# A graph layer's gather: one tile of rows in 104 fetched by SyncE row by row, the others by GpSimd

## The chip, the cores and the metric

The kernel runs on one core of a Trainium2 chip. The metric is the device time of one execution in microseconds (us); lower is better. Of a core's engines the profile names PE (TensorE, with PEld for its weight loads), DVE (VectorE), ACT (ScalarE), POOL (GpSimd) and SP (SyncE). SP computes nothing here: its queue (SPq in the profile) issues transfers.

## The reference

One layer of a graph network over 12500 nodes with 96 features and 412500 edges that are sorted by their destination node. For each edge a message is formed from the source node's features, the destination node's features and the edge's own four attributes; the messages are normalized over all edges and summed by destination node.

```python
def _mlp(h, W, b, gamma, beta):
    h = relu(h @ W + b)
    mu, var = mean(h, axis=0), mean(square(h - mean(h, axis=0)), axis=0)
    return gamma * (h - mu) * rsqrt(var + 1e-5) + beta

node_feat = _mlp(x, W_node, b_node, g_node, beta_node)
edge_feat = _mlp(edge_attr, W_edge, b_edge, g_edge, beta_edge)
message = _mlp(concat([x[src], x[dst], edge_feat], axis=1), W_msg, b_msg, g_msg, beta_msg)
agg = segment_sum(message, dst, num_segments=12500)
x = layernorm(x + agg + node_feat)
```

## The kernel before

**Tables.** The product with `W_msg` splits into three parts. `table` (L144) computes the source part for every node once into a table `p_tab` in HBM, one row of 96 floats (384 bytes) per node, and the destination part into `q_tab`. So an edge needs only its row of `p_tab`, a row of `q_tab` and its edge part.

**Tiles, groups and blocks.** 128 edges are a tile (one partition per edge), four tiles a group (`GT = 4`), four groups a block (`BG = 4`): 3223 tiles, 806 groups, 202 blocks.

**Gathers.** `gather` (L162) fetches the `p_tab` rows of a group: one indirect DMA of GpSimd for each tile, whose 128 row numbers lie in the column `src[:, k]`, one per partition (L166). The groups of the first 26 blocks (`SPILL = 104` groups, called early) are gathered while the tables and the edge statistics are worked out, and are spilled to HBM. The other 702 groups (late) are gathered into a ring of `RING = 28` tiles named `pg`; the first 28 before the main loop, every further one 28 late groups ahead of its use, at the end of the loop's step (`ahead_of`, L332 and L526).

**The main loop** (from L503) has a step for each group, in an order that puts one early block between every few late ones. The order of the instructions on SP, POOL, PE, DVE and ACT is the program's (L496). In each step `linear` (L447) multiplies the edge and destination part on PE, `message` (L455) adds the gathered rows to it on DVE (L465: `hs<-z,pg`), which is also the last use of a ring tile, and ACT applies the relu; `sums` and `add` collect the messages by node.

**What SP does in the loop.** At the first step of each block SP runs `load(s + 2)` (L387), two blocks ahead: every second block five transfers of edge attributes (L396, L397), and for each block one number read from the tile `base` into a register (L400) and two transfers of rows of `q_tab` at the address that this register gives, into one of three buffers `rhs` (L405). These two wait until PE has read that buffer for the last time. For an early block `fetch` (L408) brings its spilled rows back (L412).

Of the kernel before, what the change touches and what calls it, by code (L numbers as in the profile page):

```python
# [11 lines left out]
F32 = mybir.dt.float32  # L12
I32 = mybir.dt.int32
# [3 lines left out]
ET = mybir.EngineType  # L17
# [3 lines left out]
N, C, E, ED = 12500, 96, 412500, 4  # L21
EPS = 1e-5
P = 128
# [3 lines left out]
GT, GE, BG = 4, 512, 4  # L27
NT = -(-E // P)
NG = -(-NT // GT)
NBL = -(-NG // BG)  # L30
NTP, NGP = NBL * BG * GT, NBL * BG
EP = NGP * GE
# [23 lines left out]
SPILL = 26 * BG  # L56
RING = 28
RAW = 3
SKEW = 6
HB, RB = 3, 3  # L60
CL, CE = 2, 2
J = 8


# [12 lines left out]
def gnn(ctx, tc, t):  # L77
    nc = tc.nc
    const = ctx.enter_context(tc.tile_pool(name="const", bufs=1))
    dram = ctx.enter_context(tc.tile_pool(name="dram", bufs=1, space=DRAM))  # L80
    p_tab = dram.tile([NN, C], F32, name="p_tab")
# [11 lines left out]
    ring = rpool.enter_context(tc.tile_pool(name="ring", bufs=RING))  # L93
# [65 lines left out]
            queues[c // CH % len(queues)].dma_start(rows[:, c:c + CH, :], r)  # L159
            yield  # L160

    def gather(g, pg):  # L162
        tab, idx = (t["x"], src_raw) if g < RAW * BG else (p_tab, src)
        for i in range(min(GT, NT - g * GT)):
            k = g * GT + i
            nc.gpsimd.indirect_dma_start(  # L166
                out=pg[:, i, :], out_offset=None, in_=tab[:, :],
                in_offset=bass.IndirectOffsetOnAxis(ap=idx[:, k:k + 1], axis=0))
        return pg
# [107 lines left out]
    def edge_norm():  # L277

        with tc.tile_pool(name="es", bufs=2) as work, tc.tile_pool(name="es1", bufs=1) as one, \
                tc.tile_pool(name="es_ps", bufs=4, space=PSUM) as ps:  # L280
            stats = one.tile([P, NS, NBL, 6], F32, name="estats")
            for b in range(NBL):
                if b % J == 0:
                    yield
                    ea = work.tile([P, J, GE], F32, name="ea")
                    n = min(J, NBL - b)
                    for i in range(NS):
                        nc.sync.dma_start(ea[Q * i:Q * i + 2 * EK, :n, :],
                                          t["ea"][EK * i:EK * (i + 2), b:b + n, :])
                for i in range(NS):  # L290
                    k = NS * b + i
                    if k % 2 == 0:
                        pr = ps.tile([P, 2, GE], F32, name="pr")
                    nc.tensor.matmul(pr[:, k % 2, :], wide[Q * i:Q * i + 2 * EK, :],  # L294
                                     ea[Q * i:Q * i + 2 * EK, b % J, :], start=True, stop=True)
                    if k % 2:
# [32 lines left out]
            nc.vector.tensor_scalar(w_e, w_msg[:, 2, :], a_e, None, op0=OP.mult)  # L329

    def fast(ring):
        def ahead_of(g):  # L332
            return gather(g, ring.tile([P, GT, C], F32, name="pg"))

        with tc.manual_schedule(engines={ET.SP, ET.Pool}):
            with tc.tile_pool(name="tab_w", bufs=1) as work, tc.tile_pool(name="tab_ps", bufs=2, space=PSUM) as ps:
# [20 lines left out]
            got = {g: ahead_of(g) for g in range(SPILL, SPILL + RING)}  # L357
# [11 lines left out]
        with tc.tile_pool(name="fix", bufs=1) as fix, tc.tile_pool(name="msg", bufs=2) as work, \  # L369
# [17 lines left out]
            def load(s):  # L387

                b = order[s]
                first = SPILL // BG  # L390
                c, o = ((b - first) // CL * CL + first, CL) if b >= first else (b // CE * CE, CE)
                if c not in eas:
                    o = min(o, NBL - c)
                    eas[c] = work.tile([P, o, GE], F32, name="ea" if b >= first else "eae")
                    for i in range(BG):
                        nc.sync.dma_start(eas[c][Q * i:Q * i + EK, :, :], t["ea"][EK * i:EK * (i + 1), c:c + o, :])  # L396
                    nc.sync.dma_start(eas[c][EK:P:Q, :, :], rel_d[:, c * BG * GE:(c + o) * BG * GE]  # L397
                                      .rearrange("o (b g e) -> (o g) b e", g=BG, e=GE))
                ea = eas[c][:, b - c, :]
                _, val = nc.values_load_multi_w_load_instructions(  # L400
                    base[:, b:b + 1], engines=[ET.SP], min_val=0, max_val=N - 1,
                    skip_runtime_bounds_check_because="they are nodes' numbers")
                for i in range(2):
                    rows = q_tab[WS * i:, :][bass.ds(val[0], 4 * WS), :].rearrange("(k w) f -> w k f", k=2)
                    nc.sync.dma_start(rhs[C:C + WN, s % RB, i::2, :], rows[:WN])  # L405
                block[s] = ea

            def fetch(s):  # L408
                b = order[s]
                if b * BG < SPILL:  # L410
                    back = work.tile([P, BG, GT, C], F32, name="pb")
                    nc.sync.dma_start(back, spill[b].rearrange("p g (a c) -> p g a c", a=GT))  # L412
                    for i in range(BG):
                        got[b * BG + i] = back[:, i, :, :]
# [18 lines left out]
            def edges(s):  # L433

                prs[s] = ps.tile([P, BG, GE], F32, name="pr", bufs=1)
                for i in range(min(BG, NG - order[s] * BG)):
                    nc.tensor.matmul(prs[s][:C + WN, i, :], we[Q * i:Q * i + EK + 1, :],  # L437
                                     block[s][Q * i:Q * i + EK + 1, :], start=True, stop=True)

            def prepare(s):  # L440

                n = min(BG, NG - order[s] * BG)
                pr, x = prs[s], left[s % 2]
                nc.scalar.activation(x[:C, :n, :], pr[:C, :n, :], AF.Relu)  # L444
                nc.vector.tensor_scalar(x[C:C + WN, :n, :], pr[C:C + WN, :n, :], 0.0, None, op0=OP.is_equal)  # L445

            def linear(k):  # L447
                s, g = steps[k]
                n = min(GT, NT - g * GT)
                zs[k] = ps.tile([P, GT, C], F32, name="z")  # L450
                for i in range(n):
                    nc.tensor.matmul(zs[k][:, i, :], left[s % 2][:KR, g % BG, i * P:(i + 1) * P],  # L452
                                     rhs[:KR, s % RB, g % BG, :], start=True, stop=True)

            def message(k):  # L455
                g = steps[k][1]
                n = min(GT, NT - g * GT)
                i = g % BG
                h, z, pg = hb[k // 2 % HB], zs.pop(k), got.pop(g)
                if i % 2 == 0:  # L460
                    nc.vector.tensor_tensor(  # L461
                        h[:, :, :, C + 1:C + 1 + WN], rel[:, g:g + 2, :].unsqueeze(3).to_broadcast([P, 2, GT, WN]),
                        iota[:, i:i + 2, :].unsqueeze(2).to_broadcast([P, 2, GT, WN]), op=OP.is_equal)
                hs = work.tile([P, GT, C], F32, name="hs", bufs=3)
                nc.vector.tensor_add(hs[:, :n, :], z[:, :n, :], pg[:, :n, :])  # L465
                nc.scalar.activation(h[:, i % 2, :n, :C], hs[:, :n, :], AF.Relu)  # L466

            def sums(k):

                s, g = steps[k]  # L470
                n = min(GT, NT - g * GT)
                h = hb[k // 2 % HB][:, g % 2, :, :]
                if g % BG == 0:
                    pas[s] = ps.tile([C + 1, BG, P], F32, name="pa")
                for i in range(n):
                    r = min(P, E - (g * GT + i) * P)
                    nc.tensor.matmul(pas[s][:, g % BG, :C + 1 + WN], h[:r, i, :C + 1], h[:r, i, :C + 1 + WN],  # L477
                                     start=i == 0, stop=i == n - 1)

            def add(s):  # L480
# [9 lines left out]
                    nc.vector.tensor_tensor(to, pa[:, i:n:2, C + 1:C + 1 + WN], to, op=OP.add)  # L490
                nc.vector.tensor_add(gram[:, :n, :], pa[:, :n, :C + 1], gram[:, :n, :])  # L491

            n, ahead = len(steps), SPILL + RING
            with tc.manual_schedule(engines={ET.SP, ET.Pool, ET.PE, ET.DVE, ET.Activation}):  # L496
                load(0)
                fetch(0)
                load(1)
                edges(0)  # L500
                prepare(0)
                linear(0)
                for k in range(n + SKEW):  # L503
                    s, g = steps[min(k, n - 1)]
                    if k < n and g % BG == 0:
                        if s + 2 < len(order):
                            load(s + 2)
                        if s + 1 < len(order):
                            fetch(s + 1)
                    if k + 1 < n:  # L510
                        linear(k + 1)
                    if k < n:
                        message(k)
                    if 0 <= k - 1 < n:
                        sums(k - 1)
                    if k < n and s + 1 < len(order):
                        if g % BG == 0:
                            edges(s + 1)
                        if g % BG == 2:
                            prepare(s + 1)  # L520
                        if g % BG == 3 and order[s + 1] < RAW:
                            convert(s + 1)
                    if k >= SKEW and (k - SKEW) % BG == 0:
                        add((k - SKEW) // BG)
                    if k < n and g >= SPILL and ahead < NG:
                        got[ahead] = ahead_of(ahead)  # L526
                        ahead += 1

            d = fix.tile([C, BG, C], F32, name="d")
            s = fix.tile([C, 3], F32, name="s")  # L530
# [237 lines left out]
```

## Time and profile before

| | us |
|---|---|
| median of 3 runs | 5475.15 |
| lowest and highest of them | 5470.85 to 5479.21 |
| the profiled execution, its own time | 4143.65 |
| its span in the profile | 4141.9 |
| mean granted TensorE clock in it | 0.764 |

All durations below are of the one profiled execution, whose own time is 1331.5 us below the median. A row of the table of groups names a line, an engine, an operation and `out<-in`, then how often it ran, its busy time, the mean of one in ns, the idle time of its engine ahead of it and what ended most of that. "issue" there is time in which the engine waited for nothing that the profile shows. In a list of waits, "A <- B: t, n, m" says that A waited for B t us in total, n times, at most m us. An answer about one line gives count and the shortest, median and longest duration in ns, then the first and last start in us.

### The profile page before, as it was taken

How to read it: one execution, taken by the hardware profiler on the slowest of the kernel's cores; microseconds unless marked ns; L12 is line 12 of the kernel's file. 1: busy time of each engine (PE TensorE's matmuls, PEld its weight loads, DVE VectorE, ACT ScalarE, POOL GpSimd, SP SyncE). 2: the span in 40 equal slices, each digit the busy share in tenths (PEclk: the TensorE clock that was granted, in tenths of full speed). 3: DMA queues.
4: the chain of work that ended last, by engine and by line, in shares of the span. 5: the costliest groups of instructions: out<-in, count | busy, mean ns of one | idle time of the engine just before them, and what ended most of it. 6: DMA issues, size and time to landing. Idle time of an engine off the chain costs nothing. (4 is left out here: it accounts for less than half of the span.)

```text
span 4141.9 us, 48307 instructions
## 1 busy us (share of the span) xinstructions
PE 2736.8 (66%) x16705; PEld 2333.7 (56%) x16705; DVE 1715.8 (41%) x2837; ACT 1144.4 (28%) x1417; POOL 3063.0 (74%) x3231
## 2 busy tenths in 40 slices
PE   6699976777566656666565656655666565665666
PEld 6466645666456545555555555555555555555556
DVE  2579993444333333333333333332333333333334
ACT  0358862223222222222122222221222122222222
POOL 7677777777777777777777777777777777777772
PEclk9755556889778878877788777877877788877785
DMA  6455542222221222122212221222212212222123
GB/s 212 140 142 113 113 81 56 54 55 55 53 53 46 53 53 54 46 53 53 52 47 53 52 54 45 53 54 52 55 45 54 52 46 55 53 52 53 46 52 108
DMA packets 154615, 270.89 MB, mean 65 GB/s; under 512 B 83665, under 2 KB 84178, under 8 KB 153356
## 3 DMA queue, kind: packets, MB, share of 16 engines
q0 software_dynamic: 103136, 158.62, 16.2%
q1 hardware_dynamic: 48138, 98.39, 8.1%
q10 hardware_dynamic: 3088, 10.71, 0.8%
q8 instruction: 134, 2.20, 0.2%
q14 instruction: 119, 0.97, 0.1%
HBM read 225.88 MB, written 41.60 MB: 65 GB/s over the span
## 5 line engine op out<-in xcount | busy, mean ns | idle before, releaser
L166 POOL DMA_INDIRECT pg<-p_tab,src x2807 | 2662.4, 948 | 856.5 <-issue 705.9
L452 PE MATMUL z<-rhs,left 128*128 128x96 f32 x6446 | 1111.9, 329 | 1246.2 <-issue 1145.0
L452 PEld LDWEIGHTS z<-rhs,left 128*128 128x128 f32 x6446 | 1016.7, 240 | 1458.0 <-issue 1325.0
L466 ACT ACTIVATE h<-hs 128x384 f32<-128x384 f32 x806 | 421.3, 523 | 2613.7 <-DVE hs L465 2613.7
L465 DVE TENSOR_TENSOR hs<-z,pg 128x384 f32<-128x384 f32 x702 | 389.2, 554 | 1558.1 <-DMA pg<-p_tab,src 1308.9
L477 PE MATMUL pa<-h 128*97 128x128 f32 x6446 | 1026.0, 312 | 4.1 <-ACT h L466 4.1
L477 PEld LDWEIGHTS pa<-h 128*97 128x97 f32 x6446 | 913.4, 198 | 4.5 <-ACT h L466 4.5
L445 DVE TENSOR_SCALAR left<-pr 31x2048 f32<-31x2048 f32 x202 | 463.0, 2292 | 487.2 <-ACT left L444 487.2
L166 POOL DMA_INDIRECT stage<-p_tab,src x368 | 350.6, 953 | 131.9 <-issue 109.7
L444 ACT ACTIVATE left<-pr 96x2048 f32<-96x2048 f32 x202 | 374.0, 1851 | 16.1 <-PE pr L437 16.1
L294 PE MATMUL pr<-ea,wide 10*128 10x512 f32 x1212 | 361.4, 1073 | 9.4 <-issue 7.8
L300 DVE BATCH_NORM_STATS2 estats<-r 128x6 f32<-128x512 f32 x606 | 360.2, 676 | 9.3 <-ACT r L298 9.3
L298 ACT ACTIVATE r<-pr 128x1024 f32<-128x1024 f32 x303 | 301.9, 1024 | 113.0 <-PE pr L294 76.8
L294 PEld LDWEIGHTS pr<-ea,wide 10*128 10x128 f32 x1212 | 223.0, 314 | 146.5 <-issue 69.4
L437 PE MATMUL pr<-ea,we 6*127 6x512 f32 x1404 | 202.5, 645 | 12.2 <-DMA ea<-rel_d 12.2
L461 DVE TENSOR_TENSOR h<-rel,iota 128x248 f32<-128x248 f32 x403 | 164.3, 408 | 0.0
L465 DVE TENSOR_TENSOR hs<-z,pb 128x384 f32<-128x384 f32 x104 | 57.7, 555 | 133.4 <-PE z L452 133.4
L491 DVE TENSOR_TENSOR gram<-pa,gram 97x388 f32<-97x388 f32 x202 | 111.4, 551 | 0.0
L490 DVE TENSOR_TENSOR agg<-pa,agg 97x62 f32 x404 | 90.1, 223 | 14.4 <-PE pa L477 0.8
L154 PE MATMUL pt<-w_msg,xp 96*128 96x96 f32 x392 | 85.2, 422 | 13.8 <-DMA xp<-in_xp 9.3
L154 PEld LDWEIGHTS pt<-w_msg,xp 96*128 96x128 f32 x392 | 84.0, 332 | 14.8 <-issue 9.3
L437 PEld LDWEIGHTS pr<-ea,we 6*127 6x127 f32 x1404 | 55.1, 183 | 38.0 <-issue 13.1
(106 smaller groups left out, 591.5 us busy)
## 6 DMA issues: line engine op xcount, KB each, us to landing
pg<-p_tab,src POOLq DMA_INDIRECT x2807
spill<-stage SPq DMA_DIRECT2D x26, 768.0 KB
pb<-spill SPq DMA_DIRECT2D x26, 768.0 KB
ea<-in_ea SPq DMA_DIRECT2D x75, 160.0 KB
rhs<-q_tab SPq DMA_DIRECT2D x404, 23.2 KB
ea<-in_ea SPq DMA_DIRECT2D x352, 20.0 KB
stage<-p_tab,src POOLq DMA_INDIRECT x368
q_tab<-trow SPq DMA_DIRECT2D x7, 672.0 KB
```

The costliest lines, as they stand in the source:

```text
L154: nc.tensor.matmul(pt[:, g, :], xp[:, k:k + P], w, start=True, stop=True)
L166: nc.gpsimd.indirect_dma_start(out=pg[:, i, :], out_offset=None, in_=tab[:, :], in_offset=bass.IndirectOffsetOnAxis(ap=idx[:, k:k + 1], ax ...
L294: nc.tensor.matmul(pr[:, k % 2, :], wide[Q * i:Q * i + 2 * EK, :], ea[Q * i:Q * i + 2 * EK, b % J, :], start=True, stop=True)
L298: nc.scalar.activation(r, pr, AF.Relu)
L300: nc.vector.bn_stats(stats[:, (k - o) % NS, (k - o) // NS, :], r[:, 1 - o, :])
L437: nc.tensor.matmul(prs[s][:C + WN, i, :], we[Q * i:Q * i + EK + 1, :], block[s][Q * i:Q * i + EK + 1, :], start=True, stop=True)
L444: nc.scalar.activation(x[:C, :n, :], pr[:C, :n, :], AF.Relu)
L445: nc.vector.tensor_scalar(x[C:C + WN, :n, :], pr[C:C + WN, :n, :], 0.0, None, op0=OP.is_equal)
L452: nc.tensor.matmul(zs[k][:, i, :], left[s % 2][:KR, g % BG, i * P:(i + 1) * P], rhs[:KR, s % RB, g % BG, :], start=True, stop=True)
L465: nc.vector.tensor_add(hs[:, :n, :], z[:, :n, :], pg[:, :n, :])
L466: nc.scalar.activation(h[:, i % 2, :n, :C], hs[:, :n, :], AF.Relu)
L477: nc.tensor.matmul(pas[s][:, g % BG, :C + 1 + WN], h[:r, i, :C + 1], h[:r, i, :C + 1 + WN], start=i == 0, stop=i == n - 1)
```

## The change

For 25 of the late groups GpSimd gathers only the first three tiles. The fourth tile's 128 rows are fetched by SP: `row_numbers` brings the tile's 128 row numbers into one partition (`lin`), and `rows_of` reads ten of them into SP registers at a time and issues one transfer for each, from that row of `p_tab` to that row's partition of the ring tile. The ten go out at the end of every second step that gathers a group, so that a tile takes 26 groups of gathers (104 tiles): with the 674 groups gathered in the loop this happens 25 times (groups 132, 158, ..., 756), in 13 batches each (12 of ten rows, one of eight). The row numbers of the next such tile are fetched at the first batch of the one before it. A further input array `rows` holds the row numbers with a tile in each row.

```diff
+SR, SS = 10, 2
+SG = SS * -(-P // SR)
...
-    def gather(g, pg):
+    def gather(g, pg, without=0):
         tab, idx = (t["x"], src_raw) if g < RAW * BG else (p_tab, src)
-        for i in range(min(GT, NT - g * GT)):
+        for i in range(min(GT, NT - g * GT) - without):
...
+            def row_numbers(g):
+
+                lin = work.tile([1, P], I32, name="lin")
+                nc.sync.dma_start(lin, t["rows"][g * GT + GT - 1:g * GT + GT, :])
+                return lin
+
+            def rows_of(pg, lin, lo, hi):
+                _, val = nc.values_load_multi_w_load_instructions(
+                    lin[:, lo:hi], engines=[ET.SP], min_val=0, max_val=N - 1,
+                    skip_runtime_bounds_check_because="they are nodes' numbers")
+                for p in range(lo, hi):
+                    nc.sync.dma_start(pg[p:p + 1, GT - 1, :], p_tab[bass.ds(val[p - lo], 1), :])
...
             n, ahead = len(steps), SPILL + RING
+            lins = {ahead: row_numbers(ahead)}
...
                     if k < n and g >= SPILL and ahead < NG:
-                        got[ahead] = ahead_of(ahead)
+                        m = (ahead - SPILL - RING) % SG
+                        if m == 0:
+                            by_row = ahead if ahead + SG <= NG else None
+                        got[ahead] = ahead_of(ahead, int(ahead == by_row))
+                        if by_row is not None and m % SS == 0:
+                            if m == 0 and ahead + 2 * SG <= NG:
+                                lins[ahead + SG] = row_numbers(ahead + SG)
+                            lo = m // SS * SR
+                            rows_of(got[by_row], lins[by_row], lo, min(lo + SR, P))
                         ahead += 1
```

More of the change, by code (lines that the diff above doesn't have):

```diff
@@ L331, in fast, with ahead_of @@
     def fast(ring):
-        def ahead_of(g):
-            return gather(g, ring.tile([P, GT, C], F32, name="pg"))
+        def ahead_of(g, without=0):
+            return gather(g, ring.tile([P, GT, C], F32, name="pg"), without)
         with tc.manual_schedule(engines={ET.SP, ET.Pool}):
@@ L742 @@
     give("src", np.pad(s, (0, EP - E)).reshape(NTP, P).T)
+    give("rows", np.pad(s, (0, EP - E)).reshape(NTP, P))
     give("dst", d.reshape(NTP, P).T)
```

## The prediction

> **What bounds the kernel now.** I read the page's busy times first, then the groups, then the stretches of the loop, the answer for the gather's line, and last the waits of the engines and of SP's queue.
>
> ```profile
> PE 2736.8 (66%) x16705; PEld 2333.7 (56%) x16705; DVE 1715.8 (41%) x2837; ACT 1144.4 (28%) x1417; POOL 3063.0 (74%) x3231
> ...
> L166 POOL DMA_INDIRECT pg<-p_tab,src x2807 | 2662.4, 948 | 856.5 <-issue 705.9
> ```
>
> No engine looks full: POOL shows 74%. But its second row says that between two gathers (948 ns each) it stood for 856.5 / 2807 = 0.305 us and that this was mostly "issue", so nothing made it wait. The gap belongs to the gather.
>
> ```profile
> 1000.00:2000.00 1000.00, 621.62 (x4186) 552.54 (x4184) 346.90 (x581) 224.85 (x291) 756.70 (x799) 0.80 0.20 51
> 2000.00:3000.00 1000.00, 612.81 (x4104) 543.77 (x4104) 339.55 (x569) 217.34 (x283) 756.98 (x798) 0.79 0.20 52
> 3000.00:4000.00 1000.00, 611.52 (x4104) 543.05 (x4104) 342.82 (x572) 221.92 (x287) 756.40 (x799) 0.79 0.20 51
> ```
>
> The columns are the stretch, its length, the busy time of PE, PEld, DVE, ACT and POOL, the clock, the DMA engines' share and GB/s. In every 1000 us POOL makes 798 or 799 gathers, one in 1.2525 us, whatever mix of blocks falls into it. From the first start to the last in the trace, 3223 gathers take 4069.5 us, 1.263 us each; in the loop's phase the mean is 1.2536 us. PE is 61% busy and the DMA engines 20%.
>
> ```profile
> DVE hs L465 <- DMA pg<-p_tab,src: 1308.9, 331, 8.3
> ...
> POOL pg L166 <- DVE hs L465: 8.8, 29, 0.3
> ...
> SPq L405 <- PE z L452: 2814.1, 398, 26.0
> ```
>
> The consumer waits for the gather (1308.9 us) and the gather almost never for a free ring tile (8.8 us): POOL's queue sets the pace from start to end. The last gather starts at 4072.6 and the span ends at 4141.9, so 69 us follow it. SP, by the third line, stands for most of the loop.
>
> **What the skill says.** "Perfetto Trace Analysis", section DMA Optimizations, item 3: where descriptor generation is the bottleneck, balancing transfers over the engines that can issue them may help. The trace shows that case at POOL. "DMA: Bandwidth & Descriptors", Issuing engines are not separate DMA queues: all issuers share 16 DMA engines, and another issuer saves only sequencer time. That agrees with a DMA share of 0.20: room below, a full issuer above. The same page, Latency and other measured facts, gives a register load a floor of about 600 ns; the trace has 431 to 815 ns on SP. "Runtime: NRT & Kernel Launch", Instruction fetch mechanics, puts a bulk load at about 200 ns for each register, from HBM; no run here shows a load of several, and this one reads SBUF.
>
> **Removed.** 25 of the 2807 ring gathers leave POOL, the only engine without slack: 25 x 1.2536 = **31.3 us**. Nothing else moves past POOL; the gathers behind each come that much earlier, and the 69 us of tail follow. The consumer keeps pace, as PE is 61% busy.
>
> **Added on SP.** 3200 row transfers, 325 register loads of ten (25 of eight), 25 transfers of row numbers. The rows for the prices, each a count and shortest/median/longest in ns:
>
> ```profile
> L192 SPq DMA_DIRECT2D b_msg<-in_L_gnn_b_msg x1: 264/264/264, 15.7 to 15.7; - x1
> ...
> L377 SPq DMA_DIRECT2D rhs<-bias x12: 578/590/608, 629.4 to 636.4; - x12
> ...
> L405 SPq FUSED_REGOPS  x404: 42/46/51, 639.7 to 4019.8; - x135
> L405 SPq MOVE rhs<-q_tab x404: 29/29/42, 639.8 to 4020.0; - x135
> L405 SPq DMA_DIRECT2D rhs<-q_tab x404: 227/262/1016, 639.9 to 4021.3; - x135
> ...
> L400 SPq TENSOR_LOAD <-base x202: 431/680/815, 638.9 to 4008.7; - x101
> ```
>
> - A row transfer. Line 405 already issues transfers from HBM at an address from a register: 46 + 29 + 262 ns, and the trace has gaps of about 50 ns after each of the three: 0.49 us. A single 384-byte row from HBM (line 192) costs 264 ns by itself, so I take 0.49. Low end: 223 ns (line 193's transfer) and the same rest, 0.45. High end: line 377's row from SBUF to SBUF costs 590 ns, which would make 0.82. I take the first because source and address kind are the same.
> - A load of ten. Low end: as a load of one, 0.68 us. By the skill's figure 0.68 + 9 x 0.2 = 2.5 us, an estimate, which I take. High end: ten loads of one, 6.8.
> - The row numbers: 25 transfers of about 0.3 us, 8 us in all.
>
> Sum: 3200 x 0.49 + 325 x 2.5 + 8 = 1568 + 813 + 8 = **2389 us** on SP.
>
> What covers it: the batches are spread over the time from the first loop gather to group 780, 2575 gathers, or 3228 us. In the trace from 1000 to 3900 us SP waits 2428.9 of 2900 us at line 405 alone, 84%; so 0.84 x 3228 = 2704 us are free there. 2389 fit into that, at 88% of it; with the 16% that SP does now it is then (0.16 x 3228 + 2389) / 3228 = **90% busy**. The limit lies at 2704 / 3200 = 0.845 us for each row with its share of the load; my price is 0.75.
>
> Order on SP: in each block the waiting `load` comes first, then the two batches, then the next block's `load`. The batches need nothing from PE or DVE, except the first of a tile, which waits for `hs` of the group that used the ring tile before (its own step). Behind SP is the next `load`, two blocks ahead of use (some 40 us at 16 x 1.25 = 20 us for a block), so being late by less than a block delays nobody. A tile's last batch goes out four groups, about 20 us, ahead of its `hs`. Even a late row would not hold POOL: the ring is 28 groups deep, and the consumer has 39% to catch up with. So I cost the new wait of `hs` on SP's rows, and the few semaphore waits it needs (17 ns each on DVE, 25 times), at nothing; the cover is DVE's 1308.9 us of waiting. On the DMA engines 3200 packets of 384 bytes are added to 154615.
>
> **Sum for the profiled execution:** 4143.65 - 31.3 = 4112.3 us, span 4110.6. The median of the runs is 1331.5 us higher, and the profile does not say where. If that time lies outside the gathers, 31 us go (5444). If each gather is that much slower, 1.656 us, 25 x 1.656 = 41.4 us go (5434). A time that scales with the length of the kernel is easier to put into 3223 equal gathers than anywhere else I see, so I lean to the second: **5437 us**. In that reading SP also has more room, unless it is slower in the same ratio.
>
> **Rivals.**
> 1. *SP becomes the bound (slower).* Place: SP's queue in the loop. From 0.845 us for a row with its share of load, SP can't finish two batches and its `load` within a late block's 20 us; the lag adds up until `rhs` comes late and PE waits. Price at the high row end: (0.82 x 3200 + 813) - 2704 = 733 us over, or with short loads 2624 + 221 - 2704 = 141 over; in the middle about 430, less the 31. That is some 5870 us on the median's scale (5585 to 6180). For it: my own 90%, and line 377's 590 ns. Against: source and address are those of line 405, at 262 ns. 0.17.
> 2. *Rows land too slowly (slower, the same place).* SP's transfers take turns on eight completion semaphores, as the trace shows at each, and one waits for the one eight before it. If a row takes over 8 x 0.59 = 4.7 us to land, the pitch passes the limit. No wait of that kind is long now (1.9 us once). It is in the 0.17.
> 3. *Contention gives the gain back (same).* If SP's transfers stretch each of the other 2782 gathers by 31.3 / 2782 = 0.011 us, 0.9%, nothing is left: 5475. For it: some gathers do take up to 1237 ns where the median is 947. Against: the pitch holds at 1.25 us through stretches with and without SP's 768 KB transfers. 0.06.
> 4. *The change doesn't do what it says:* that the three gathers of such a group take POOL as long as four. Each gather is an instruction of its own, so I see no way.
>
> **How the numbers follow.** Faster 0.77, same 0.06, slower 0.17; 0.2% is about what a measurement of this kernel can tell from no change (11 us). The range takes the likeliest case with both scales of the gain (5434 to 5444), the spread of the runs (about 4 us either way) and partial losses up to no gain: 5420 to 5476. The slower rival is left out.
>
> **What would show it.** Right: 2782 ring gathers at an unchanged 948 ns and 0.305 us of gap; the span 31 us shorter; row transfers of about 260 ns at starts some 0.49 us apart; SP's wait at line 405 down from 2814 to some 450 us; PE's and DVE's waits of the same kinds as now. Wrong: SP's wait at line 405 near zero and new waits of PE at line 452 for `rhs` (rival 1), SP waiting for its own rows (rival 2), or gaps above 0.305 us at line 166 (rival 3). A load of ten above 3.4 us, or a row above 0.59 us, would overturn the sum; so would POOL waiting for `hs`.

## The result: 1.2% slower

| | before | after |
|---|---|---|
| median, us | 5477.18 | 5544.65 |
| lowest to highest, us | 5470.85 to 5482.49 | 5534.80 to 5552.47 |
| executions | 4 | 4 |
| ratio of after to before | | 1.0123, 95% interval 1.0104 to 1.0141 |

The change costs 67 us where I forecast a gain of 38. The profiled execution of after took 5552.47 us by its own time, with a span of 5550.7 us. It is like the other executions of its kernel. The execution of before from which I made the prediction was not: its 4143.65 us were not seen again, for all 80 other executions of that kernel took between 5407 and 5498 us. So the profile after is set beside a new profile of the unchanged kernel (the first experiment, span 5455.6 us). In the changed kernel the gather is line 168, `z` line 454, `hs` line 467, the `rhs` transfers line 407, the load of ten registers line 502 and the row transfers line 506.

From the page of after, the busy times and the gathers' row of the groups:

```profile
PE 3114.1 (56%) x16705; PEld 2511.7 (45%) x16705; DVE 1723.7 (31%) x2837; ACT 1139.3 (21%) x1417; POOL 3037.3 (55%) x3206
...
L168 POOL DMA_INDIRECT pg<-p_tab,src x2782 | 2638.4, 948 | 1957.6 <-DVE hs L467 1143.5
```

The 25 gathers are gone and one still takes 948 ns. But POOL is busy for 55% of the span, and most of what it stands idle for is now `hs`: it waits for a free ring tile. In the profile that I read, that wait was 8.8 us. (133.2 us of the 1143.5 are one wait, for the loop's first `hs`.)

The stretches of the loop of after (stretch, length, busy time and instructions of PE, PEld, DVE, ACT and POOL, clock, DMA share, GB/s):

```profile
2000.00:3000.00 1000.00, 557.87 (x3288) 474.17 (x3289) 274.45 (x459) 176.24 (x229) 593.19 (x626) 0.71 0.18 40
3000.00:4000.00 1000.00, 559.07 (x3266) 474.32 (x3265) 269.91 (x451) 175.66 (x227) 594.40 (x628) 0.70 0.18 41
```

POOL gets 626 or 628 gathers into 1000 us, not 798, and no other engine is busier for it. From the waits of the engines in after (who waited for what, us in total, times, longest):

```profile
DVE hs L467 <- issue: 1760.0, 262, 14.7
...
PE z L454 <- issue: 1300.5, 349, 19.1
POOL pg L168 <- DVE hs L467: 1143.5, 288, 133.2
...
DVE hs L467 <- DMA pg<-p_tab,src: 109.6, 40, 2.8
```

The same two lines in the profile that I read were:

```profile
PE z L452 <- issue: 1145.0, 201, 11.9
...
DVE hs L465 <- issue: 96.9, 42, 2.8
```

The consumer's wait for gathers has shrunk from the 1308.9 us of that profile to 109.6. In its place DVE stands for 1760 us, not 97, for which the profile shows no releaser at all. PE's line tells little: it was 1145 us already. SP's part of the change, asked for by line in after (count and shortest/median/longest in ns, first and last start in us), and SP's own waits:

```profile
L506 SPq MOVE pg<-p_tab x3200: 1/29/1422, 1065.6 to 5242.8; - x189
L506 SPq DMA_DIRECT2D pg<-p_tab x3200: 1/225/1407, 1065.7 to 5242.9; - x189
...
L502 SPq TENSOR_LOAD <-lin x325: 3/1207/2442, 1064.1 to 5232.5; - x163
```

```profile
SPq L407 <- PE z L454: 183.9, 45, 24.7
...
SPq L506 <- DMA pg<-p_tab: 52.9, 91, 1.4
```

A row's transfer costs a median of 225 ns, the move ahead of it 29 (but up to 1422), and a load of ten 1207; these medians are under the prices that I had put on them. Yet SP's wait for `rhs` to come free has all but gone: within a batch the starts of neighbouring rows lie a mean of 0.92 us apart (median 0.56), not the 0.49 that I forecast.

### The profile page after: what moved, and what is told of

It reads as the page before. It is cut to its first block, busy times and chain, and to the rows that moved or that the text cites. A ratio compares the mean times of both kernels' runs of the same rounds, so it can differ in the third digit from the quotient of the medians.

```text
span 5550.7 us, 58501 instructions
## 1 busy us (share of the span) xinstructions
PE 3114.1 (56%) x16705; PEld 2511.7 (45%) x16705; DVE 1723.7 (31%) x2837; ACT 1139.3 (21%) x1417; POOL 3037.3 (55%) x3206
## 5 line engine op out<-in xcount | busy, mean ns | idle before, releaser
L168 POOL DMA_INDIRECT pg<-p_tab,src x2782 | 2638.4, 948 | 1957.6 <-DVE hs L467 1143.5
L454 PE MATMUL z<-rhs,left 128*128 128x96 f32 x6446 | 1201.1, 342 | 1358.4 <-issue 1300.5
L454 PEld LDWEIGHTS z<-rhs,left 128*128 128x128 f32 x6446 | 1088.2, 252 | 1606.8 <-issue 1524.1
L479 PE MATMUL pa<-h 128*97 128x128 f32 x6446 | 1234.0, 335 | 553.8 <-issue 550.6
L479 PEld LDWEIGHTS pa<-h 128*97 128x97 f32 x6446 | 1031.3, 214 | 640.5 <-issue 639.9
L296 PE MATMUL pr<-ea,wide 10*128 10x512 f32 x1212 | 403.8, 1074 | 314.8 <-issue 220.3
L296 PEld LDWEIGHTS pr<-ea,wide 10*128 10x128 f32 x1212 | 204.8, 321 | 512.4 <-issue 340.6
L439 PE MATMUL pr<-ea,we 6*127 6x512 f32 x1404 | 229.2, 724 | 15.5 <-DMA ea<-rel_d 12.6
```

The lines of the kernel that those rows point to most:

```text
L168: nc.gpsimd.indirect_dma_start(out=pg[:, i, :], out_offset=None, in_=tab[:, :], in_offset=bass.IndirectOffsetOnAxis(ap=idx[:, k:k + 1], ax ...
```

## Experiments

Ratios are to the kernel before on the same chip, with 95% intervals. Where two experiments are compared, their ratios are, since the kernel before takes 5441 to 5487 us on different chips. What is read from a trace is one execution.

**1. The kernel before again.** No edit.

> The kernel before, unchanged, for a trace of it at the time of the median (5477 us) and not of the one execution of 4144 us that the prediction read. Theory A (in the timed executions the consumer of the gathers, not POOL, sets the pace): about 5477 us, POOL waits for DVE hs (ring tiles in use) for over 800 us in sum, and the mean distance of two gathers in the loop is near 1.6 us while single gathers still take 948 ns. Theory B (POOL sets the pace there too, each gather being slower): about 5477 us, POOL's wait for DVE hs stays under 50 us and the gather's own 948 ns or its 0.305 us gap has grown by 0.4 us.

Measured: 0.9994 (0.9972 to 1.0016), 5445 us. From the waits of its engines:

```profile
DVE hs L465 <- remote: 1447.4, 168, 15.5
...
POOL pg L166 <- DVE hs L465: 1024.2, 194, 131.7
...
PE z L452 <- issue: 856.4, 561, 9.3
```

So the unchanged kernel, too, has POOL waiting for `hs` for 1024 us (131.7 of them in one wait, for the loop's first `hs`), and DVE standing for 1447 us at a wait whose releaser the profile can't name ("remote"). What happens there is seen in its timeline (start, duration, engine, line, operation, count, and the idle time ahead with its releaser):

```profile
3030.77 1.92 PE L477 MATMUL pa<-h 128*97 128x128 f32 x8
...
3033.98 0.45 PEld L477 LDWEIGHTS pa<-h 128*97 128x97 f32 x2
3034.04 0.95 POOL L166 DMA_INDIRECT pg<-p_tab,src  x1 [0.31 <-issue]
...
3034.95 0.37 PE L477 MATMUL pa<-h 128*97 128x128 f32 x1 [0.40 <-issue]
...
3035.66 0.37 PE L477 MATMUL pa<-h 128*97 128x128 f32 x1 [0.33 <-issue]
...
3037.07 0.52 PE L477 MATMUL pa<-h 128*97 128x128 f32 x1 [1.04 <-issue]
3037.79 0.95 POOL L166 DMA_INDIRECT pg<-p_tab,src  x1 [0.30 <-issue]
3038.45 0.24 PEld L477 LDWEIGHTS pa<-h 128*97 128x97 f32 x1 [1.17 <-issue]
3039.04 0.94 POOL L166 DMA_INDIRECT pg<-p_tab,src  x1 [0.30 <-issue]
...
3041.97 0.24 PEld L477 LDWEIGHTS pa<-h 128*97 128x97 f32 x1 [1.17 <-issue]
...
3042.73 1.02 DVE L465 TENSOR_TENSOR hs<-z,pg 128x384 f32<-128x384 f32 x2 [11.09 <-remote]
...
3043.56 0.95 POOL L166 DMA_INDIRECT pg<-p_tab,src  x1 [3.58 <-DVE hs L465]
```

From about 3033.5 on, PE's matmuls and weight loads, 8 of which take 1.9 us at 3030.77, start 0.7 us or a multiple of it apart, though they wait for nothing. In other such stretches a register move of SP takes 0.7 us as well. POOL's gathers go on at 1.25 us as if nothing were wrong, until the ring is full and POOL has to wait for `hs`. Some 2.7 us after POOL's last gather has ended, the others run at full speed again, and then POOL too. I call such a stretch *crawling*. Counted in the trace as stretches of over 2 us in which every matmul of PE starts over 0.5 us after the one before it and has no semaphore wait of its own, it fills 967 us of this kernel's loop, 656 us of the changed one's, and nothing in the execution of 4143.65 us. That count is no measure of time lost (below, the removal alone has 959 us of it, and the run with fixed addresses only 477 and yet takes longer), only of whether crawling is there. The loop itself (first ring gather to last `hs`) takes 4599 us here and 4691 in after: the loss is in the loop.

Not all that sets this execution apart from the one that I read lies in the loop. The first ring gather starts at 790.2 us here and at 555.0 there, so that 235 us of the 1314 between the two spans are lost ahead of it, where GpSimd gathers the early groups. The loop, 3521 us there, accounts for 1079.

**2. The removal alone.** The 25 gathers are left out, and SP brings 128 fixed rows of `p_tab` by one transfer.

```diff
-            lins = {ahead: row_numbers(ahead)}
...
-                        if by_row is not None and m % SS == 0:
-                            if m == 0 and ahead + 2 * SG <= NG:
-                                lins[ahead + SG] = row_numbers(ahead + SG)
-                            lo = m // SS * SR
-                            rows_of(got[by_row], lins[by_row], lo, min(lo + SR, P))
+                        if ahead == by_row:
+                            nc.sync.dma_start(got[by_row][:, GT - 1, :], p_tab[:P, :])
```

> The changed kernel with the removal alone: GpSimd leaves out the same 25 gathers, and SP fetches the fourth tile of those groups by one transfer of 128 fixed rows (rows 0 to 127 of the table) and not by 128 row transfers, so those edges get other rows' values. Theory A (POOL isn't the bound in the timed executions): within 12 us of the kernel before, 5465 to 5489. Theory B (POOL is the bound, the gain of the removal is real and SP's transfers cost more than it): 31 to 42 us faster than before, 5435 to 5446.

Measured: 0.9945 (0.9931 to 0.9958), 5417 us, 29 us less: 1.18 us for each gather taken away. Theory A (within 12 us) is out; the interval, 23 to 38 us, reaches into theory B's 31 to 42, but POOL waits for `hs` for 1025 us in this run as well, so B's reason doesn't hold either. That a gather is worth its time all the same fits the crawling: while POOL gathers at full pace the others hardly move, while they move POOL stands, and so the two times add up rather than overlap.

**3. The rows alone.** POOL gathers everything; SP also fetches its 3200 rows, into a spare tile that nobody reads.

```diff
-                    nc.sync.dma_start(pg[p:p + 1, GT - 1, :], p_tab[bass.ds(val[p - lo], 1), :])
+                    nc.sync.dma_start(pg[p:p + 1, 0, :], p_tab[bass.ds(val[p - lo], 1), :])
...
+            spare = fix.tile([P, 1, C], F32, name="spare")
...
-                        got[ahead] = ahead_of(ahead, int(ahead == by_row))
+                        got[ahead] = ahead_of(ahead)
...
-                            rows_of(got[by_row], lins[by_row], lo, min(lo + SR, P))
+                            rows_of(spare, lins[by_row], lo, min(lo + SR, P))
```

> The kernel before with SP's part of the change alone: GpSimd gathers every tile, and SP also fetches the 3200 rows into a spare tile that nothing reads. Theory A (SP's instructions cost, the removal gives nothing): about as the changed kernel, 5535 to 5560. Theory B (removal worth 31 to 42): that much above the changed kernel, 5575 to 5590. A third possibility, that the consumer's wait for SP's rows costs the time: 5477 as before, since nobody waits for the spare tile.

Measured: 1.0315 (1.0255 to 1.0376), 5609 us, 163 us more by the medians and more than any of the three expectations. No instruction that computes depends on these rows, so what costs is that SP issues them. Between the removal alone and the whole change the rows cost less, 1.0123 - 0.9945 = 0.0178 or 97 us. From the page, the row of `hs` for the early groups, whose spilled rows SP brings back (`pb`):

```profile
L467 DVE TENSOR_TENSOR hs<-z,pb 128x384 f32<-128x384 f32 x104 | 56.7, 554 | 217.5 <-DMA pb<-spill 125.9
```

At 11 of the 26 early blocks the first `hs` starts 5 to 7 us after SP has issued the block's `fetch`, and had waited 126 us for it in all: SP is late. In the changed kernel the spilled rows cost `hs` 14 us of waiting, but it also waits for the change's own rows. At four of the 25 tiles `hs` starts 1.2 to 1.6 us after SP has issued the last row, after waits of 45 us in sum. (The list of waits has only 3.6 us of this under the rows' own name; the rest it puts down to other transfers of SP, which use the same semaphores.) Waits of `hs` for SP's transfers, then, make 126 us here and some 60 in the changed kernel. In the unchanged kernel, in the removal alone and in the next two runs there are none. Why SP is later here than in the changed kernel stays open.

**4. Rows from fixed addresses.** The changed kernel, with each of the 3200 rows taken from row `p` of the table: no register loads, no moves and no address instructions.

```diff
...
-                    nc.sync.dma_start(pg[p:p + 1, GT - 1, :], p_tab[bass.ds(val[p - lo], 1), :])
+                    nc.sync.dma_start(pg[p:p + 1, GT - 1, :], p_tab[p:p + 1, :])
...
```

> The changed kernel with the same 3200 row transfers, but at fixed rows of the table (row p for partition p): no register loads, no address instructions, so 3200 added SP instructions and not some 9900; the 25 tiles hold other rows. Theory S (in these runs the engines' queues stall together for microseconds while GpSimd gathers, each instruction of any queue then takes a slot of 0.7 us, and the cost goes by added SP instructions): of the 97 us that the rows cost beside the removal a third, 31 us; with the removal's -29 about 0 against before, from -15 to +20 us. Theory T (the cost goes by transfers, through their landing or their semaphores): all of it, +55 to +80 us. Theory Q (SP has too little time of its own, and its late rhs costs): SP's own time falls by half and with it all of the cost, -20 to -35 us.

Measured: 0.9974 (0.9964 to 0.9984), 5474 us. The same number of transfers of the same size costs 0.0029 against the removal alone, 16 us (7 to 25) where the change's rows cost 97. So 3200 small transfers and their completions are not what costs: theory T is out. (The fixed rows also lie side by side, which the change's don't.) The total against before, 14 us less (9 to 20), lies at the edge of theory S's range and just short of theory Q's, that SP has too little time of its own; with the late transfers of the run before, Q stays in play.

**5. Ten rows in a transfer.** As the run with fixed addresses, with one transfer for each batch.

```diff
...
-                for p in range(lo, hi):
-                    nc.sync.dma_start(pg[p:p + 1, GT - 1, :], p_tab[bass.ds(val[p - lo], 1), :])
+                nc.sync.dma_start(pg[lo:hi, GT - 1, :], p_tab[lo:hi, :])
...
```

> As the one with fixed addresses, but the ten rows of a batch go by one transfer: 325 added instructions and transfers for the same bytes and rows at the same places of the program. Theory S and theory T: nearly nothing is left of the cost, -20 to -35 us against before, as with the removal alone (-29). A cost that goes by rows or descriptors of 384 bytes would leave +50 to +80.

Measured: 0.9935 (0.9919 to 0.9952), 5452 us: no different from the removal alone. With 325, 3200 and 9925 added instructions on SP (3200 x 3 and 325 loads in the change) the cost is none, 16 and 97 us. It grows with SP's instructions, and with the time that they take of SP, but not in proportion.

**6 and 7. The kernel before with a slower gather.** One or three small memsets of GpSimd into a tile of its own behind each loop gather. They are there to test whether the crawling comes from the gathers' pace.

```diff
             nc.gpsimd.indirect_dma_start(
...
+            if pace is not None:
+                for _ in range(3):
+                    nc.gpsimd.memset(pace, 0.0)
```

> The kernel before with a pause behind each gather of the ring in the main loop: GpSimd fills a tile of 64 columns with zeros (one instruction, about 0.1 to 0.2 us). Theory S (the stream of gathers at 1.25 us brings the stalls, and the time of the gathers and that of the consumer add up because of them): fewer stalls, the time falls by 50 to 600 us although POOL has more to do. If POOL's own work were the bound: 2695 x 0.1 to 0.2 = 270 to 540 us slower. If the stalls don't depend on the pace of the gathers: within 30 us of before, since POOL waits for ring tiles anyway.

> The same with three such instructions behind each gather (0.3 to 0.6 us). Theory S: the stalls are gone or nearly, POOL sets the pace again, and the time is near 4144 + 2695 x (0.3 to 0.6) = 4950 to 5760 us, POOL's wait for DVE hs under 200 us. POOL the bound already: 800 to 1600 us slower. Stalls independent of the pace: slower by at least what is over the 1.607 us that a gather takes now on average.

Measured: one memset 1.0028 (1.0017 to 1.0039), 5502 us; three 1.0898 (1.0879 to 1.0916), 5980 us. One memset hides in the gap after the gather: the median time from start to start is 1.280 us, and crawling still fills 827 us. By itself this is what was expected if the crawling didn't depend on the pace. Three memsets make it 1.682 us, and PE's crawling is gone, though the time is above the 4950 to 5760 us of theory S. From the waits of the engines with three:

```profile
ACT h L472 <- DVE hs L471: 3883.7, 743, 9.6
DVE hs L471 <- DMA pg<-p_tab,src: 2874.1, 556, 9.3
```

The consumer waits for gathers again, and POOL hardly for `hs`: at this pace POOL is the bound that I had taken it for all along.

**8. The changed kernel with three memsets.** The same edit made in the changed kernel.

> The changed kernel with three small memsets of GpSimd behind each loop gather, as in the run with three memsets (1.0898 of the kernel before, 5980 us). Theory S (what the rows cost is the time for which all queues crawl while gathers run at their closest pitch; without those stretches SP's added instructions lie beside other work): the 25 gathers less bring 25 x 1.82 = 45 us against that run and the rows cost nothing, so 5935 us, 1.082 of the kernel before; SP waits at line 407 for most of the loop, POOL hardly waits for hs. Theory R (the added SP instructions or their transfers cost time whatever the pace, as the 67 us of the change say net): 5980 + 67 = 6047 us, 1.102.

Measured: 1.0951 (1.0923 to 1.0979), 5960 us. This ran on another chip, one on which the kernel before takes 46 us less. In microseconds it is 20 less than the run before it, by the ratios 0.0053 (29 us) more, and the loops in the two traces take 5109.7 us here and 5119.4 there. By none of the three is it the 45 us less of theory S or the 67 more of theory R. How much of the net loss is gone, this pair doesn't settle; the last pair below, on one chip, is the better one.

**9 and 10. Two memsets.** The kernel before with two memsets behind each gather, of 128 x 64 and of 128 x 4.

> The kernel before with two memsets of 128 x 64 behind each loop gather. One memset left the pitch median at 1.28 us and the stretches of crawling in place (5502 us), three made it 1.68 and removed them (mean 1.82). Two should give a median of about 1.48. Theory S: the crawling is gone or much less, POOL sets the pace, and the loop takes 2807 x (1.48 + 0.14) = 4550 us, with some 860 around it 5410 us (0.986 of the kernel before); if the crawling stays, the time is above that of one memset, 5510 to 5700 us.

> The same with two memsets of 128 x 4, which are shorter; pitch median 1.35 to 1.4 us. Theory S with a threshold below that pitch: 2807 x (1.38 + 0.14) + 860 = 5130 us (0.935). With the threshold above it the crawling stays and the time is near that of one memset, 5500 us (1.003). A value between says that the crawling lessens with the pitch and doesn't end at one value.

Measured: two large ones 0.9933 (0.9908 to 0.9959), 5410 us, the expected time, though not the expected ratio of 0.986, as this chip's kernel before takes less; two small ones **0.9526 (0.9504 to 0.9549), 5187 us**, 254 us faster than the kernel before, the best of all runs here. From the groups of GpSimd in the run with two small memsets (count, busy time and mean ns, idle time ahead and what ended it), and a stretch of its loop:

```profile
L166 POOL DMA_INDIRECT pg<-p_tab,src x2807 | 2685.4, 957 | 908.5 <-issue 463.7 <-DMA rhs<-q_tab 132.1 <-DVE hs L471 11.5
L171 POOL MEMSET pace<- 128x4 f32 x5390 | 582.5, 108 | 157.4
```

```profile
3000.00:4000.00 1000.00, 555.45 (x3398) 491.85 (x3397) 284.21 (x472) 183.32 (x237) 779.61 (x1993) 0.71 0.20 44
```

POOL spends 582 us more on useless memsets, its wait for `hs` is 11.5 us (besides the one long wait at the start of the loop, 132.1 us, which the profile puts down to `rhs` here), and the kernel is faster. The memsets stand only in the loop: the first ring gather still starts at 783.0 us. The five paces side by side, all of the kernel before; median and mean are the time from one ring gather's start to the next:

| memsets behind each gather | median, us | mean, us | crawling, us | ratio |
|---|---|---|---|---|
| none | 1.252 | 1.607 | 967 | 0.9994 |
| one, 128 x 64 | 1.280 | 1.622 | 827 | 1.0028 |
| two, 128 x 4 | 1.367 | 1.544 | 0 | 0.9526 |
| two, 128 x 64 | 1.473 | 1.627 | 0 | 0.9933 |
| three, 128 x 64 | 1.682 | 1.823 | 0 | 1.0898 |

The crawling ends between 1.28 and 1.37 us, and past that point the time follows the pace. A memset that fits into POOL's gap changes little, and two or three that lengthen it end the crawling: this shows that in these executions the crawling hangs on how POOL's gathers follow each other. It doesn't show by what means. Nor does it tell the distance of the gathers from the number of instructions between them, since the runs with the longer distance are those with two memsets and more. And a close pace alone doesn't bring crawling: the execution of 4143.65 us kept 1.251 us and had none.

**11 and 12. The change at the best pace.** The changed kernel and the kernel before, both with two memsets of 128 x 4, on one chip.

> The changed kernel with two memsets of 128 x 4 behind each loop gather, to stand beside the unchanged one with the same memsets on the same chip (5187 us before, 0.953). Theory S in full (rows cost only through the crawling, which this pace removes): 25 x 1.54 = 39 us less than its partner, 5148. Theory S in part, as the run with three memsets suggests (POOL's pauses between gathers came to 32 us more with the rows, so that 10 of 42 us were left): 0 to 15 us less than its partner, 5175 to 5187. Theory R (added SP instructions cost what they cost in the changed kernel): 67 us more than its partner, 5254.

> The kernel before with two memsets of 128 x 4 behind each loop gather again, as the partner of the run beside it: 0.953 of the kernel before, 5187 us on a chip where that takes 5441.

Measured: 0.9556 (0.9520 to 0.9592), 5196 us, with the change; 0.9544 (0.9511 to 0.9577), 5194 us, without it. The ratios differ by 0.0012 (-0.0037 to 0.0061, which is 20 us less to 33 us more). So at this pace the change is worth nothing that can be seen either way, and both the 39 us less of theory S in full and the 67 more of theory R are out. The removal should bring 39 us (25 x 1.55, an estimate), and then the rows take about as much, give or take 27. POOL's pauses beyond the median pace (sum over all gathers of start to start, less the median) are 529 us with the change and 497 without: 32 of the 39 us are given back there. Part of it can be read in the gathers' line, first with the change, then without it:

```profile
L168 POOLq EVENT_SEMAPHORE  x800: 17/17/28965, 41.7 to 5121.3; - x160
```

```profile
L166 POOLq EVENT_SEMAPHORE  x700: 17/17/28502, 41.5 to 5121.2; - x175
```

Each of the 25 ring tiles into which SP wrote puts four more semaphore waits on POOL ahead of a later gather. Those gathers start a median of 2.20 us after the one before, the first gathers of other groups 1.85: 25 x 0.35 = 9 us. Most of the rest is that the other first gathers come a little later as well (a mean of 1.90 us against 1.84, 650 of them: 36 us), less some 12 us at gathers that wait for no semaphore. PE doesn't crawl in either run.

## Why the prediction was wrong, step by step

- **What bounds the kernel now** is the step that failed first. Its reading was right for the execution shown: POOL without a wait, 798 gathers in 1000 us. But that execution was 1331.5 us below the median, and I carried the bound over to executions in which POOL makes 647 gathers in 1000 us and waits for `hs` for 1024 us. My sentence that a time scaling with the length is easiest to put into "3223 equal gathers" was a guess, and wrong: the gathers take the same 949 ns. Of the missing time 235 us lie ahead of the loop; in the loop it is 1079 us, and POOL's waits for `hs` are nearly as long. The prediction itself named POOL's wait for `hs` as what would overturn the sum, and the new profile of the unchanged kernel has it.
- **Removed** came close, by luck: 29 us (23 to 38) measured for the removal alone, 31.3 to 41.4 forecast, but from a bound that wasn't there. A gather on an engine that waits is still worth 1.18 us, which fits a consumer that crawls while it runs.
- **Added on SP**, the unit prices. A row transfer at full speed is 0.41 us from start to start (median with three memsets) where I took 0.49 from line 405. The load of ten I took at 2.5 us, by the figure of the Trainium skill, "Runtime: NRT & Kernel Launch", Instruction fetch mechanics, for loads from HBM. It has two durations, and its median hides that: with three memsets the even batches (0, 2, ... 10) take a median of 1.20 us, the odd ones 2.32, and the last, of eight, 0.79. With 0.68 us for a load of one, each further register costs (2.32 - 0.68) / 9 = 0.18 us from SBUF in the odd batches, near the page's 0.2, and 0.06 in the even ones; why they alternate I can't say. (The 17 ns for a semaphore wait on DVE was misread: ahead of `hs` it is a median of 50.) At full speed SP's room was sized well enough: an estimate from these durations and rows a mean of 0.43 us apart is 1.9 ms for what SP adds, where I had 2.4. In the timed executions rows lie a mean of 0.92 us apart, over the 0.59 that the prediction named as overturning its sum.
- **The cover**, costed at nothing, is the term of the sum that turned the gain into a loss: -29 us for the removal and +97 for what SP does make about the measured 67. I held that a tile's last batch goes out about 20 us ahead of its `hs` and that lateness delays nobody. In the changed kernel `hs` waits some 60 us for late transfers of SP, which itself crawls. Whether the other part is time that SP's instructions take from the other engines, no run shows by itself. At the pace without crawling about 40 us (give or take 27) of the 97 are left.
- **Rival 1**, SP as the bound, gave the right sign and was right in part: SP hardly waits in the loop any more (184 us for PE at `rhs`, where it was 2814), and some of its transfers come late. But the late ones are the spilled rows and the last rows of a tile. The `rhs` transfers still go out ahead of need (in after, from the second block on, never less than 11.8 us before PE uses them), and the loss is about a tenth of its price. **Rival 2**: SP waits 52.9 us for its own rows; small. **Rival 3**, dearer gathers: 948 ns as before. It is right in the last pair of runs, where the gain is given back on POOL, but by pauses between groups and not by contention. The page "DMA: Bandwidth & Descriptors" of the skill, Issuing engines are not separate DMA queues, is not contradicted: the DMA engines' share was 0.18, and ten rows in a transfer cost nothing.

What stays open: by what means close gathers hold up the other queues, whether SP's instructions lengthen that or only come late because of it, and why it didn't occur in the one execution of 4143.65 us. Whether that depends on the recording of the trace was not tried. That the 57 us between 97 and 40 are crawling is argued from the two paces, not measured by itself.

## What to carry to other kernels

Before reading a profile for its bound, hold its time against the median: an execution a quarter faster than all others answers for another kernel. If an engine's waits end in "issue" or "remote" where another profile had a named releaser, and one engine's queue goes on all the same, look in the timeline for a common step between instructions, and try slowing that engine before taking work from it. An idle issuing engine is not free: cost its added instructions by a run with the instructions alone, and look there for consumers that wait for its other transfers. Before a median goes into a price, look whether the durations fall into two groups.

## What I had not expected of the hardware

- While indirect gathers of 128 rows of 384 bytes follow each other at 1.25 us, instructions of PE and SP start 0.7 us or a multiple of it apart for microseconds on end, in all executions looked at but one. With two memsets between the gathers, one in 1.37 us, PE's don't.
- Two memsets of 108 ns behind each gather made the kernel 4.7% faster.
- 3200 transfers of one row cost 16 us with fixed addresses, and 97 with addresses from registers and the loads of these.
- A load of ten registers from SBUF takes 1.20 or 2.32 us, by turns from batch to batch.
- With two small memsets behind each gather, the first gather of a group, which has a semaphore wait of 17 ns ahead of it, comes 0.46 us later than the others (1.83 against 1.37 from start to start). Without memsets the same wait adds nothing to the median (1.252 against 1.251, in the unchanged kernel's new profile).
